# Layer 1 of a two-layer attention kernel: products, values and softmax sums in one TensorE tile mode

## The chip, the cores and the metric

The kernel runs on one core of a Trainium2 chip. The metric is the time of one execution in device microseconds (us). Before the change it is 3169.02 us, the median of three runs (3168.06 to 3169.51).

## The reference

The input x is one image of 256 x 256 tokens with 128 channels, fp32. Two layers are computed, each on a group-normalised copy of x and added to x. What the functions below leave out is the scaling of inputs and the reshapes between image and rows.

```python
# layer 0: rows of 256 tokens, 8 heads of 32, with a gate and a bias from pairs
bias = jnp.einsum('nijz,zh->nhij', pair_repr, bias_proj)[:, None]
gate = jax.nn.sigmoid(msa_repr @ gate_proj)
q, k, v = jnp.split(msa_repr @ qkv_proj, 3, axis=-1)
sim = jax.nn.softmax(jnp.einsum('nsqhc,nskhc->nshqk', q, k) * scale, axis=-1) + bias
out = (jnp.einsum('nshqk,nskhc->nsqhc', sim, v) * gate).reshape(bs, s, r, cm) @ out_proj

# layer 1: rows of 256 tokens, 4 heads of 64, each token sees 16 to either side
qkv = x2 @ w_in.T + b_in
q, k, v = (heads(t) for t in jnp.split(qkv, 3, axis=-1))
scores = jnp.einsum('bhid,bhjd->bhij', q, k) / jnp.sqrt(D)
scores = jnp.where(jnp.abs(i - j) <= band, scores, -jnp.inf)      # band = 16
out = jnp.einsum('bhij,bhjd->bhid', jax.nn.softmax(scores, axis=-1), v)
y = out.transpose(0, 2, 1, 3).reshape(B * T, F, C) @ w_out.T + b_out
```

In both layers a row has 256 tokens and 256 channels, and there are 128 rows (S = 128, R = C = 256). All arithmetic is in fp32.

## The kernel before

Layer 0 takes the first 2090 us of the span and is not touched by the change; a final check of the softmax sums follows layer 1. Names in the code: P is 128 (partitions), A is 4, B is 32, KB is 64 (keys of one block of the band), NB is 4 (such blocks in a row), and `strip(n)` is the partitions 32n to 32n + 31.

**Products of a row.** A 256 x 256 by 256 x 256 product is not done as eight quarter products but as seven, of sums and differences of quarters (`Seven`, and in layer 1 `Summed`). `Quarters` holds the weights' quarters and their sums. The sums of the inputs are made by GpSimd (`row_sums`: tile 1ts from 1xn for q and k, tile 1att from 1at for the output product o). Each of the seven products is one call of `nc.tensor.matmul` with a 128 x 128 stationary operand and 256 moving columns (L594). An fp32 matmul shows in the trace as two matmuls and two weight loads. `in_turn` takes the three streams q, k and o together: product n of q, of k, of o, each followed at once by its take (L655 to L685: a copy or an addition from PSUM, by ScalarE for q and k, by VectorE with the residual for o, by VectorE for the additions). That gives 21 products in a pass, named p1q, p1k and p1o.

**One pass of layer 1** works on two rows; the loop is `for i in range(last)` and runs 63 times. A pass counts here from its first p1q. In it TensorE does, in this order:

- the 21 products of `stretch`: q and k of the next pair of rows, o of an earlier pair;
- `values` (L1045): the values v of the next two rows, p1v, token by channel. Two column halves of the array, 128x64, take the keys of the two halves of a block of 64 tokens for half of the heads each, over four blocks and two input halves, with 128 moving columns;
- `scores` (L1066): 1sim, in 64x64 tiles with 96 moving columns, band blocks only. ScalarE then takes exponentials (L1074), GpSimd masks them (L1076, tile 1p) and adds those of even and odd blocks (L1083, tile 1zp);
- `attend` (L1107): 1av of the pair before, in 64x64 tiles, then 1zs (L1119): the sums of the softmax weights over keys, by a stationary operand `place` of zeros and ones. Each half of the partitions of 1zp is a half of the heads and goes to its own bank, in eight 64x32 tiles; `place` has ones in columns 0 to 15 for the lower half and 16 to 31 for the upper half, so that each bank holds the sums of one half of the heads and zeros for the other.

ScalarE copies the first bank of 1zs to 1z (L1130), and VectorE adds the second (L1131). VectorE takes reciprocals in three parts (L1144), the second and third between the takes of the next products. Then SyncE sends them to DRAM (L1152, rz_far) and back, spread over partitions (L1156, 1near), and loads a coming pair of rows (L741, yg). VectorE multiplies 1av with 1near (L1176, 1at), and 1av, of which there is one buffer, is free again. VectorE's transposes (L1219) and SyncE's stores (L1229) follow for finished rows.

**What sets the order.** In layer 1 the whole order on all engines is written out (`manual_schedule`): instructions run on each engine in the order of the program's text, and waits are placed where tiles demand them. PSUM banks for products and values come from a ring, here of four (`psum(lay, "1", 4, 0)`, L972); the other four banks are 1av's two and 1zs's two.

The last rows, after the loop, use `one_by_one` (L708, 1po) for their output product, with plain quarter products.

Of the kernel before, what the change touches and what calls it, by code (L numbers as in the profile page):

```python
# [9 lines left out]
F32 = mybir.dt.float32  # L10
# [29 lines left out]
def conv_preact_kernel(  # L40
# [525 lines left out]
    def row_sums(t, x, engine):  # L566
# [3 lines left out]
        engine.tensor_tensor(t[:, 2], x[:, 3], x[:, 2], ALU.subtract)  # L570
        engine.tensor_tensor(t[:, 3], x[:, 1], t[:, 1], ALU.subtract)

    class Seven:


        def __init__(self, pool, weights, x, t, name, tag, by_token=False):
            self.weights, self.x, self.t, self.by_token, self.name = weights, x, t, by_token, name
# [7 lines left out]
        def product(self, n, two=None, first=False):  # L585
            x, t = self.x, self.t
            moving = {1: x[:, 0], 2: x[:, 1], 3: x[:, 3], 4: t[:, 3], 5: t[:, 0], 6: t[:, 1], 7: t[:, 2]}[n]
            out = two if n == 2 else self.ps[:, 1 if n in (3, 5) else 0, :]

            first = first or n == 1  # L590
            flags = dict(stop=n in (2, 3, 4), skip_group_check=True)
            weights = self.weights.stationary(n)
            if not self.by_token:
                nc.tensor.matmul(out, lhsT=weights, rhs=moving, start=first, **flags)  # L594
                return
            for t2 in range(2):
                cols = slice(t2 * P, (t2 + 1) * P)
                nc.tensor.matmul(out[:, cols], lhsT=moving[:, cols], rhs=weights, start=first and t2 == 0, **flags)  # L598

        def take(self, what):  # L600
            if what == "15":
# [44 lines left out]
            p.add_mid()  # L646

    class Summed(Seven):

# [47 lines left out]
            if n in (1, 5):  # L699
                amid(n)  # L700

    def one_by_one(w, at, name, done):

        ps = proj_bank(name)
        done(ps)
        for m in range(2):
            for kt in range(2):
                nc.tensor.matmul(  # L708
                    ps[:, m, :], lhsT=w[:, kt, m * P : (m + 1) * P], rhs=at[:, kt, :],
                    start=(kt == 0), stop=(kt == 1),  # L710
                )
                yield
# [10 lines left out]
    with ExitStack() as both:  # L723
# [20 lines left out]
        with ExitStack() as lay0:  # L744
# [140 lines left out]
            def stretch(names, i, s, rest=lambda: None):  # L885

                po = iter(())
                if s >= 0:
                    po = one_by_one(out_sb, st[s]["at"], f"po{s}", lambda ps: st[s].update(po=ps))
                if 2 * i >= S:  # L890
                    rest()
                    for _ in po:
                        pass
                    return
                f, g = (
                    Seven(row, quarters[w], xns[i], tss[i], f"{w}{i}", w, by_token=(w == "v")) for w in names
                )
                for w, p in zip(names, (f, g)):
                    res[w, i] = p.to
                two_of_them(row, f, g, f"{names}{i}", po, rest)  # L900


            with tc.manual_schedule(engines={mybir.EngineType.PE, mybir.EngineType.Activation, mybir.EngineType.DVE}):
                for s in range(2):
                    normal(s)
                sum_rows(0)
                stretch("qk", 0, -1)
                for s in range(2, 4):
                    normal(s)
                stretch("vg", 0, -1)  # L910
                sum_rows(1)
                most1 = Most(st1, stats1, 3, 1)
                for s in range(S):
                    scores(s, 0)()
                    zs = sum_heads(s - 1)
                    join_tiles(s, 0, 0)
                    divide(s - 1, zs)
                    if s % 2 == 0:
                        e = res["g", s // 2]
                        nc.scalar.activation(e, e, AF.Exp, scale=-1.0)  # L920
                    z = hd[s - 1, "z"][0] if s > 0 else None
                    rest = ((0, 2), (1, 0), (1, 2))
                    if s < S - 1:
                        attend(s - 1)
                        last_exp = scores(s, 1)
                        if s == 4:
                            for weights in quarters1.values():
                                weights.sum()
                        stretch(("qk", "vg")[s % 2], s // 2 + 1, s - 1, last_exp)
                        for half, j in rest:  # L930
                            join_tiles(s, half, j)
                        least(s - 1, z)
                        if s >= S - 3:
                            most1.join(s - S + 3)
                        normal(s + 4)
                        if s % 2 == 1:
                            sum_rows((s + 3) // 2)
                        finish(s - 1)
                    else:

                        scores(s, 1)()
                        for half, j in rest:
                            join_tiles(s, half, j)
                        least(s - 1, z)
                        attend(s - 1)
                load1(0)
                load1(1)
                warm = proj_bank("warm")

                def keep_on(n):  # L950

                    for _ in range(n):
                        nc.tensor.matmul(warm[:, 0, :], lhsT=ident, rhs=out_sb[:, 0, :], start=True, stop=True)

                divide(S - 1, sum_heads(S - 1))
                last_z = hd[S - 1, "z"][0]
                attend(S - 1)
                for s in (S - 2, S - 1):
                    if s == S - 1:
                        keep_on(4)  # L960
                    for _ in one_by_one(out_sb, st[s]["at"], f"po{s}", lambda ps: st[s].update(po=ps)):
                        pass
                    finish(s)
                mean1, rstd1 = channel_columns(st1, most1, 1, keep_on)
                least(S - 1, last_z)
# [3 lines left out]


        with ExitStack() as lay:
            ps_av = psum(lay, "1", 4, 0)  # L972
            row = lay.enter_context(tc.tile_pool(name="row1", bufs=4))
            att = lay.enter_context(tc.tile_pool(name="att1", bufs=2))
            st, hd, outs = {s: {} for s in range(S)}, {}, {}
# [38 lines left out]
            def project(s):  # L1014

                if s < 0:
                    return iter(())
                return one_by_one(w_out_t, st[s]["at"], f"1po{s}", lambda ps: st[s].update(po=ps))

            ats, ats_t, outputs, last_ots = {}, {}, {}, {}  # L1020

# [15 lines left out]
            def values(s):  # L1037
                if s >= S:
                    return
                i, r = divmod(s, 2)  # L1040
                ps = proj_bank(f"p1v{s}").rearrange("p a (b c) -> p (a b) c", c=P)
                for b in range(NB):
                    for kt in range(2):
                        for half in range(2):
                            nc.tensor.matmul(  # L1045
                                ps[KB * half : KB * (half + 1), b, :],
                                lhsT=xns[i][:, 2 * r + kt, KB * b : KB * (b + 1)],
                                rhs=w_in_t[:, kt, 2 * C + P * half : 2 * C + P * (half + 1)],
                                start=(kt == 0), stop=(kt == 1),
                            )  # L1050
                v = row.tile([P, NB, P], F32, tag="v", name=f"1v{s}")
                nc.scalar.copy(v, ps)  # L1052
                st[s]["v"] = v
# [32 lines left out]
            def attend(i):  # L1086
# [6 lines left out]
                    av = [av[:, half] for half in range(2)]  # L1093
                else:
                    av = [proj_bank(f"1av{i}_{half}") for half in range(2)]
                zs = ps_av.tile([P, 2, 2, R], F32, tag="zs", name=f"1zs{i}", bufs=1)
                zps = []
                for r in range(2):
                    (p, zp), v = hd.pop(2 * i + r), st[2 * i + r]["v"]
# [13 lines left out]
                                )  # L1113

                for r in range(2):
                    for half in range(2):
                        for j in range(2):
                            keys = slice(KB * half, KB * (half + 1))
                            nc.tensor.matmul(  # L1119
                                zs[strip(2 * j + r), half, 0, :], lhsT=place[keys, :], rhs=zps[r][keys, j, :],  # L1120
                                start=True, stop=True,
                            )
                hd["av", i] = (av, zs)

            def sums(i):
                if i < 0:
                    return
                zs = hd["av", i][1]
                z = att.tile([P, R], F32, tag="z", name=f"1z{i}")
                nc.scalar.copy(z, zs[:, 0, 0, :])  # L1130
                nc.vector.tensor_tensor(z, zs[:, 1, 0, :], z, ALU.add)  # L1131
                rz = att.tile([P, R], F32, tag="rz", name=f"1rz{i}")
                near = att.tile([P, 2, 2, R], F32, tag="near", name=f"1near{i}", bufs=1)
                hd["z", i] = (z, rz, near)
# [388 lines left out]
```

## Time and profile before

| What | Value |
|---|---|
| Median of three runs | 3169.02 us |
| Span of the profiled execution, first to last instruction | 3173.6 us (4.6 us above the median; the profile gives no other time of that execution) |
| Layer 0 | 0 to about 2092 us |
| The 63 passes of layer 1 | 2092.7 to about 3122 us, 16.37 us each at the median |
| TensorE matmuls and weight loads | 36,859 each |
| TensorE, VectorE, ScalarE, GpSimd busy in 2092 to 3122 us | 1025, 661, 550 and 736 us of 1030 |
| 1near transfers | 124 of 256 KB |
| Granted TensorE clock | 0.991 |

A profile's line of a group gives line, engine, operation, the tile written and the tiles read, the tile mode (rows*columns), the shape of the operand and the count, then busy time and mean duration, then the idle time before it and what ended that. Starts are measured; ends of matmuls are modelled, so that the distance from start to start tells the cost of a matmul, and its duration doesn't. "issue" as a releaser means that the profile shows nothing that the engine waited for. In the list of DMA queues q8 and q14 carry instructions of the engines, and q1 data.

### The profile page before, as it was taken

How to read it: one execution, taken by the hardware profiler on the slowest of the kernel's cores; microseconds unless marked ns; L12 is line 12 of the kernel's file. 1: busy time of each engine (PE TensorE's matmuls, PEld its weight loads, DVE VectorE, ACT ScalarE, POOL GpSimd, SP SyncE). 2: the span in 40 equal slices, each digit the busy share in tenths (PEclk: the TensorE clock that was granted, in tenths of full speed). 3: DMA queues.
4: the chain of work that ended last, by engine and by line, in shares of the span. 5: the costliest groups of instructions: out<-in, count | busy, mean ns of one | idle time of the engine just before them, and what ended most of it. 6: DMA issues, size and time to landing. Idle time of an engine off the chain costs nothing.

```text
span 3173.6 us, 87645 instructions
## 1 busy us (share of the span) xinstructions
PE 3097.4 (98%) x36859; PEld 2384.0 (75%) x36859; DVE 2558.2 (81%) x4140; ACT 1870.3 (59%) x4064; POOL 1613.4 (51%) x1651
## 2 busy tenths in 40 slices
PE   7889999999999999999999999999999999999997
PEld 5567777777777777777777777768888888888886
DVE  4669999999999999999999999956666666666665
ACT  4656666666666666666666666645555555555553
POOL 3034444444444444444444444347777777777774
PEclk8989999999999999999999999999999999999999
DMA  9931111111111111111111111004444444444343
GB/s 379 424 109 42 41 41 34 41 35 39 37 35 41 35 39 37 38 38 35 41 34 37 39 37 39 28 28 102 96 101 101 93 99 102 100 97 101 91 100 69
DMA packets 357105, 242.44 MB, mean 76 GB/s; under 512 B 276072, under 2 KB 342112, under 8 KB 350560
## 3 DMA queue, kind: packets, MB, share of 16 engines
q1 hardware_dynamic: 355808, 234.39, 27.1%
q8 instruction: 292, 4.78, 0.6%
q0 software_dynamic: 752, 2.36, 0.2%
q14 instruction: 109, 0.89, 0.1%
q10 hardware_dynamic: 144, 0.00, 0.0%
HBM read 169.09 MB, written 67.62 MB: 75 GB/s over the span
## 4 chain that ended last, share of the span: by engine, by line
PE 91%; DMA 5%; DVE 2%; ACT 1%; issue 0%; POOL 0%; SPq 0%; DVEq 0%; POOLq 0%; ACTq 0%
PE sim L784 9%; PE p1v L1045 7%; PE po L708 7%; PE av L816 7%; PE bv L816 7%; PE p1q L594 6%; PE pv L598 6%; PE p1o L594 6%; PE pq L594 6%; PE p1k L594 6%; PE pk L594 5%; PE pg L594 5%; DMA pr<-in_L_conv_pair_repr_dram 4%; PE zs L830 4%; PE 1sim L1066 3%; PE 1av L1107 3%
## 5 line engine op out<-in xcount | busy, mean ns | idle before, releaser
L797 ACT ACTIVATE ex<-sim 128x512 f32<-128x512 f32 x1024 | 547.5, 605 | 429.9 <-PE sim L784 429.9
L806 DVE TENSOR_TENSOR both<-ex 128x512 f32<-128x512 f32 x512 | 483.9, 984 | 77.0 <-ACT ex L797 77.0
L846 DVE RECIPROCAL d<-d 128x512 f32<-128x512 f32 x128 | 429.2, 3353 | 4.4
L611 POOL TENSOR_TENSOR v<-v,twovg 128x256 f32<-128x256 f32 x64 | 75.4, 1179 | 548.0 <-ACT twovg L630 548.0
L784 PE MATMUL sim<-q,k 32*128 32x256 f32 x4096 | 295.7, 401 | 1.1 <-ACT ex L797 1.1
L708 PE MATMUL po<-at,out_sb 128*128 128x256 f32 x1024 | 285.0, 382 | 4.0 <-DVE at L864 4.0
L784 PEld LDWEIGHTS sim<-q,k 32*128 32x128 f32 x4096 | 186.7, 184 | 102.4 <-issue 95.0
L816 PE MATMUL bv<-bias_sb,v 128*32 128x256 f32 x4096 | 244.5, 379 | 0.7 <-DVE t L861 0.7
L816 PE MATMUL av<-ex,v 128*32 128x256 f32 x4096 | 244.5, 379 | 0.0
L1045 PEld LDWEIGHTS p1v<-w_in_t,1xn 128*64 128x64 f32 x4096 | 222.3, 137 | 21.5 <-PE p1k L594 20.2
L1045 PE MATMUL p1v<-w_in_t,1xn 128*64 128x128 f32 x4096 | 237.7, 274 | 0.3 <-POOL place L980 0.3
L1076 POOL TENSOR_TENSOR 1p<-1ex,seen 128x768 f32<-128x768 f32 x127 | 230.9, 1818 | 13.4 <-ACT 1ex L1074 13.4
L668 ACT ACTIVATE 1q<-p1q,bqk 128x256 f32<-128x256 f32 x192 | 91.1, 474 | 244.4 <-PE p1q L594 244.4
L708 PEld LDWEIGHTS po<-at,out_sb 128*128 128x128 f32 x1024 | 185.7, 191 | 25.4 <-issue 4.3
L1176 DVE TENSOR_TENSOR 1at<-1av,1near 128x512 f32<-128x512 f32 x128 | 82.6, 686 | 148.6 <-DMA 1near<-rz_far 116.7
L816 PEld LDWEIGHTS bv<-bias_sb,v 128*32 128x32 f32 x4096 | 133.2, 110 | 88.7 <-issue 1.1
L611 POOL TENSOR_TENSOR q<-q,twoqk 128x256 f32<-128x256 f32 x64 | 47.6, 744 | 298.5 <-ACT twoqk L630 298.5
L816 PEld LDWEIGHTS av<-ex,v 128*32 128x32 f32 x4096 | 133.2, 110 | 87.8 <-issue 0.3
L766 DVE TENSOR_SCALAR xn<-xt,mean,rstd 128x256 f32<-128x256 f32 x256 | 179.9, 742 | 0.0
L1083 POOL TENSOR_TENSOR 1zp<-1p 128x512 f32<-128x512 f32 x127 | 162.1, 1276 | 10.0
L568 POOL TENSOR_TENSOR 1ts<-1xn 128x256 f32<-128x256 f32 x64 | 47.0, 734 | 234.3 <-ACT 1xn L1006 234.3
L1052 ACT COPY 1v<-p1v 128x512 f32<-128x512 f32 x128 | 75.1, 587 | 135.1 <-PE p1v L1045 131.6
(300 smaller groups left out, 7872.4 us busy)
## 6 DMA issues: line engine op xcount, KB each, us to landing
pr<-in_L_conv_pair_repr_dram SPq DMA_DIRECT2D x32, 1024.0 KB
xs<-in_x_dram SPq DMA_DIRECT2D x16, 2048.0 KB
x<-o SPq DMA_DIRECT2D x64, 512.0 KB
yg<-x SPq DMA_DIRECT2D x64, 512.0 KB
out_dram<-1o SPq DMA_DIRECT2D x256, 128.0 KB
xg<-in_x_dram SPq DMA_DIRECT2D x252, 128.0 KB
1near<-rz_far SPq DMA_DIRECT2D x124, 256.0 KB
rz_far<-1rz SPq DMA_DIRECT2D x124, 4.0 KB
```

Of the source, the lines that this page charges most:

```text
L594: nc.tensor.matmul(out, lhsT=weights, rhs=moving, start=first, **flags)
L598: nc.tensor.matmul(out[:, cols], lhsT=moving[:, cols], rhs=weights, start=first and t2 == 0, **flags)
L708: nc.tensor.matmul(ps[:, m, :], lhsT=w[:, kt, m * P : (m + 1) * P], rhs=at[:, kt, :], start=(kt == 0), stop=(kt == 1),)
L766: nc.vector.tensor_scalar(xns[i][:, 2 * r + half, :], xt[:, half, :], mean0[:, half : half + 1], rstd0[:, half : half + 1], op0=ALU.subtra ...
L784: nc.tensor.matmul(sims[j][:, kt, :], lhsT=k[p0 : p0 + D0, 2 * r + half, kt * P : (kt + 1) * P], rhs=q[p0 : p0 + D0, 2 * r + half, :], sta ...
L797: nc.scalar.activation(ex[:, j], sims[j], AF.Exp, scale=1.0 / math.sqrt(D0))
L806: nc.vector.tensor_tensor(both[:, j : j + 2], ex[:, j : j + 2, 0, :], ex[:, j : j + 2, 1, :], ALU.add)
L816: nc.tensor.matmul(to[D0 * j : D0 * (j + 1), half, :], lhsT=v[:, 2 * r + half, c0 : c0 + D0], rhs=weights(4 * half + j, kt), start=(kt == ...
L846: nc.vector.reciprocal(d, d)
L1045: nc.tensor.matmul(ps[KB * half : KB * (half + 1), b, :], lhsT=xns[i][:, 2 * r + kt, KB * b : KB * (b + 1)], rhs=w_in_t[:, kt, 2 * C + P * ...
L1076: engine.tensor_tensor(p.rearrange("p j (r c) -> p (j r) c", c=WROW)[:, :, 0 : 2 * WSTEP] .rearrange("p r (t c) -> p r t c", c=WSTEP)[:, : ...
L1083: engine.tensor_tensor(zp, p[:, :, 0:R], p[:, :, R : 2 * R], ALU.add)
```

## The change

In layer 1 the products, the values and the sums of softmax weights all use the tile mode 128x32, four tiles beside each other, each with a stationary operand of 32 columns:

- a helper `in_columns` splits a matmul into four of 32 columns. `Summed` has WIDTH = 32, so that each of the 21 products is four matmuls; `Seven`, which layer 0 uses, keeps 128. `one_by_one` takes the width as an argument: 128 in layer 0, 32 in layer 1;
- `values` writes the four strips of the partitions with four tiles of 32 tokens instead of two of 64;
- 1zs takes all 128 partitions as the contraction, with four matmuls of 32 columns in place of eight. The columns of `place` keep the two halves of the heads apart, so that one bank holds the sums of both. The addition at L1131 goes, and ScalarE's copy alone fills 1z;
- the bank that 1zs gives up goes to the ring, five instead of four.

The order of the instructions stays as written. In layer 1 a wait that sat on one matmul now sits on the first of its four.

```diff
+    def in_columns(out, lhsT, rhs, width, **flags):
+
+        for c0 in range(0, P, width):
+            cols = slice(c0, c0 + width)
+            nc.tensor.matmul(out[cols], lhsT=lhsT[:, cols], rhs=rhs, **flags)
+
     class Seven:
 
+        WIDTH = P
...
             if not self.by_token:
-                nc.tensor.matmul(out, lhsT=weights, rhs=moving, start=first, **flags)
+                in_columns(out, weights, moving, self.WIDTH, start=first, **flags)
                 return
...
     class Summed(Seven):
 
+        WIDTH = B
...
-    def one_by_one(w, at, name, done):
+    def one_by_one(w, at, name, done, width):
...
-                nc.tensor.matmul(
-                    ps[:, m, :], lhsT=w[:, kt, m * P : (m + 1) * P], rhs=at[:, kt, :],
+                in_columns(
+                    ps[:, m, :], w[:, kt, m * P : (m + 1) * P], at[:, kt, :], width,
                     start=(kt == 0), stop=(kt == 1),
                 )
...
-            ps_av = psum(lay, "1", 4, 0)
+            ps_av = psum(lay, "1", 5, 0)
...
-                        for half in range(2):
+                        for n in range(A):
+                            half, keys = n // 2, KB * b + B * (n % 2)
                             nc.tensor.matmul(
-                                ps[KB * half : KB * (half + 1), b, :],
-                                lhsT=xns[i][:, 2 * r + kt, KB * b : KB * (b + 1)],
+                                ps[strip(n), b, :],
+                                lhsT=xns[i][:, 2 * r + kt, keys : keys + B],
                                 rhs=w_in_t[:, kt, 2 * C + P * half : 2 * C + P * (half + 1)],
...
-                zs = ps_av.tile([P, 2, 2, R], F32, tag="zs", name=f"1zs{i}", bufs=1)
+                zs = ps_av.tile([P, 2, R], F32, tag="zs", name=f"1zs{i}", bufs=1)
...
                 for r in range(2):
-                    for half in range(2):
-                        for j in range(2):
-                            keys = slice(KB * half, KB * (half + 1))
-                            nc.tensor.matmul(
-                                zs[strip(2 * j + r), half, 0, :], lhsT=place[keys, :], rhs=zps[r][keys, j, :],
-                                start=True, stop=True,
-                            )
+                    for j in range(2):
+                        nc.tensor.matmul(
+                            zs[strip(2 * j + r), 0, :], lhsT=place, rhs=zps[r][:, j, :], start=True, stop=True
+                        )
...
-                nc.scalar.copy(z, zs[:, 0, 0, :])
-                nc.vector.tensor_tensor(z, zs[:, 1, 0, :], z, ALU.add)
+                nc.scalar.copy(z, zs[:, 0, :])
```

## The prediction

> **What bounds the kernel now.** I read the page first, for the busy shares and the chain that ended last.
>
> ```profile
> span 3173.6 us, 87645 instructions
> PE 3097.4 (98%) x36859; PEld 2384.0 (75%) x36859; DVE 2558.2 (81%) x4140; ACT 1870.3 (59%) x4064; POOL 1613.4 (51%) x1651
> q8 instruction: 292, 4.78, 0.6%
> PE 91%; DMA 5%; DVE 2%; ACT 1%; issue 0%; POOL 0%; SPq 0%; DVEq 0%; POOLq 0%; ACTq 0%
> ```
>
> TensorE is busy 98% of the span and carries 91% of the chain; the 5% of DMA lies at the start. So what counts is TensorE's time in layer 1, of which 63 passes last 16.37 us each. Queue q8 I keep for later: 292 packets of 16 KB, and TensorE ran 2 x 36,859 matmuls and weight loads and about 670 semaphore instructions, 74,387 in all. 74,387 / 292 is 255, so one q8 packet is a block of 256 TensorE instructions. Next, TensorE's waits in the passes (engine, line, waited for: total, times, longest).
>
> ```profile
> PE 1av L1107 <- DVE 1at L1176: 0.7, 2, 0.4
> PE 1av L1107 <- issue: 0.2, 1, 0.2
> ```
>
> Less than 3 us of waits in 1000: no other engine's lateness bounds the passes. Then TensorE's timeline over one pass (start, duration, engine, line, tile, shape).
>
> ```profile
> 2501.01 0.59 PE L594 MATMUL p1k<-1ts,sums_1k 128*128 128x256 f32 x2
> 2501.44 0.64 PE L594 MATMUL p1o<-1att,sums_1o 128*128 128x256 f32 x2
> 2501.92 0.59 PE L594 MATMUL p1q<-1ts,sums_1q 128*128 128x256 f32 x2
> ...
> 2505.41 0.59 PE L594 MATMUL p1o<-1at,sums_1o 128*128 128x256 f32 x2
> 2505.94 3.71 PE L1045 MATMUL p1v<-w_in_t,1xn 128*64 128x128 f32 x64
> 2509.58 1.56 PE L1066 MATMUL 1sim<-1q,1k 64*64 64x96 f32 x61
> ...
> 2511.64 1.30 PE L1107 MATMUL 1av<-1p,1v 64*64 64x96 f32 x54 [0.22 <-issue]
> 2512.87 0.66 PE L1119 MATMUL 1zs<-1zp,place 64*32 64x256 f32 x16
> 2513.46 0.70 PE L594 MATMUL p1q<-1xn,w_in_t 128*128 128x256 f32 x2
> 2514.00 0.59 PE L594 MATMUL p1k<-1xn,w_in_t 128*128 128x256 f32 x2
> ```
>
> Starts count here, since ends are modelled. Every fp32 product is two passes through the array, 0.43 us together, and a loss shows as a longer step: 0.48 after the sixth and seventh p1o, 0.53 from p1o to p1v, 0.54 for the first p1q. And in this pass 1av stopped for 0.47 us (2511.17 to 2511.64) "<-issue", which is no semaphore.
>
> [...] each change costs 0.09 to 0.14 us more than a steady step. [...] the trace's loads last 190, 137 and 110 ns for 128, 64 and 32 columns, 0.84 ns a column, so an uncovered load costs about 104, 51 or 24 ns here. [...]
>
> **Part by part.** Each q, k and o product is 4 matmuls of 32 columns instead of one. Layer 0 has the price: bv in 128x32 with 256 columns,
>
> ```profile
> 1509.52 1.91 PE L816 MATMUL bv<-bias_sb,v 128*32 128x256 f32 x32
> 1511.24 1.91 PE L816 MATMUL av<-ex,v 128*32 128x256 f32 x32
> ```
>
> 32 matmuls in 1.72 us, 216 ns per four, which is exactly one 128x128 pass. So 21 products stay at 9.07 us, but become 336 instructions at 27 ns where they were 84 at 108. The values (p1v) go from 64 to 128 matmuls of 128 columns. No row has 128x32 at 128 columns; I take today's time, 3.50 us (109 ns for each two become 109 for each four, 13.7 ns an instruction). Below, nothing speaks for a gain, since the columns streamed are the same; above, [...] 0 to 0.51 us a pass, kept for the range. 1zs falls from 16 to 8 pairs in the same 0.43 us.
>
> What falls away is changes of mode, since q, k, o, values and sums are then one mode: first p1q 240 ns (136 on its start, 104 for the load before its second pass), p1o to p1v 144 (93 and 51), and two late 128-column loads in the p1o stream 86 (43 each; a 32-column load is 80 ns shorter). That is 470[...]: 0.455 us a pass. p1v to sims and 1av to 1zs stay. Over 62 intervals -28.2 us, and the first three stretches, without p1o to wait behind, give -1.5.
>
> The DVE addition at L1131 (425 ns) stays off the path: DVE waits 2.2 us before it and later for the transfer 1near, 116.7 us in 50 waits. It moves the first part of the reciprocal, but parts two and three follow takes of p1q, p1k and p1o, so rz_far, 1near and 1at hardly move. ACT's copy waits on the same 1zs. The fifth bank of the ring saves nothing where TensorE waits for nothing. No DMA is added or moved past another in its queue. With a pass shorter by 0.46, 1av begins at 14.04 us of the pass instead of 14.37, and 1at, which frees its bank, ends there at 12.7 to 14.85: about 6.5 us of waits in place of 3.3, +3.
>
> So far -27. Now the instructions. A pass had 506 TensorE instructions (250 pairs and 6 semaphores), two blocks; it gets 870, 3.4 blocks. The window with the stalled pass's packet, 2.5 us long, says
>
> ```profile
> DMA  8998989999988953533519000000000030000011
> q8 instruction: 1, 0.02, 2.6%
> ```
>
> one packet, 2.6% of 16 engines for 2.5 us, so 1.04 us, in the midst of 1near and yg, which fill the DMA engines to nine tenths. It ran from 2509.35 to 2510.40, and its first instruction started at 2511.64, 1.25 us after its end. In another pass, 2560 instructions on (ten blocks), 1.43 us after the end came a smaller stall; nowhere in the passes is the lag under 1.25. So a block is usable about 1.35 us after its packet. Supply, counted from the instruction 256 ahead of the block: the packet starts 1.5 us later (mean of 11 passes, 0.2 to 2.8) if that instruction lies in the first half of p1v, which meets 1near and yg, 0.4 in the second half; it takes 1.1; with 1.35, 3.9 and 2.9 us. [...] I charge 0.4: 4.3 and 3.3.
>
> Cover is the time that 256 instructions take: today at least 2.64 us (sims and 1av at 10.3 ns, with 0.3 of mode changes), but mostly over 4, as half a block is p1v at 27 ns. After, p1v, sims and 1av are 512 instructions in 6.4 us, and each pass has just one block begun in p1v: cover 3.3 on average in its first half, 3.0 in its second. Stall 1.0 in half the passes, 0.3 in the other half; and in 3 passes of 10 a block begun in the last 80 instructions of q, k, o misses by some 0.6. Together 0.5 + 0.15 + 0.2 = 0.85 us a pass, 53 us over 62.
>
> Sum: 3173.6 - 28.2 - 1.5 + 3 + 53 = 3199.9 on the profile's own execution; its span lies 4.6 above the median of the runs, so **3195 us**.
>
> **Rivals.** (1) Instruction fetch keeps up: [...] the sum without the 53 is 3169 - 27 = 3142. For it: over 74,000 instructions lost 0.6 us this way, and layer 0 takes its blocks at 27 ns without a stall. Against: nowhere today do 512 instructions follow at 10 to 14 ns. This is the other side; it decides where supply falls under the cover of 3.0 to 3.3 us, that is if the packet isn't held up by 1near. (2) Half the stall, 0.45 us a pass: 28 - 27, 3170, no change. (3) Starvation feeds on itself: both the block begun in p1v and the one before it late, by 1.5 to 2 us a pass, as delays of 2.8 occur already: 3169 - 27 + 93 to 124, 3235 to 3266. (4) Fetch harmless, but p1v at 125 ns for four: 3142 + 32 = 3174; this is TensorE's own issue as the bound.
>
> **Numbers.** Main case 0.48 (3178 to 3215 its own range); fetch harmless 0.22; half stall 0.08; heavy starvation 0.14; dearer p1v alone 0.08. 0.2%, about what a measurement of this kernel tells from no change, is 6.3 us. Faster is (1) and a little of (2): 0.24; same, most of (2) and part of (4): 0.08; slower, the rest, 0.68. Range 3141 to 3240: it takes in most of (1) and the near end of (3).
>
> **What would show it.** In the profile after: first p1q to p1k 0.43 instead of 0.54, p1o to p1v about 0.43 and p1o steps of 0.43 without 0.48 show the modes saved; p1v in 3.5 us shows its price; "issue" gaps inside p1v, sims or 1av, after q8 packets that start late under 1near, show the starvation, with q8 near 380 packets. I am wrong if those gaps are absent (then 3142), or if they are there and a pass still comes out under 16.3 us; and if 1av's waits on 1at reach some 0.5 us a pass, rather than 0.1, the bound has moved to the transfer.

## The result, and the profile after

The changed kernel takes 3220.02 us, the median of four runs (3219.54 to 3224.32), beside 3169.27 us for the kernel before: a ratio of 1.0159, 95% interval 1.0145 to 1.0174. It is slower by 51 us, where the forecast was 26.

The profiled execution has a span of 3218.4 us, 44.8 more than that of before (this profile lies 1.6 us under the median of its runs, that of before 4.6 above its own). From the page, in the order in which the lines of before were shown:

```profile
span 3218.4 us, 111797 instructions
PE 3093.7 (96%) x48525; PEld 2250.4 (70%) x48525; DVE 2533.0 (79%) x4076; ACT 1870.9 (58%) x4064; POOL 1616.3 (50%) x1651
q8 instruction: 383, 6.28, 0.8%
PE 90%; DMA 5%; issue 2%; DVE 2%; ACT 1%; POOL 0%; SPq 0%; DVEq 0%; POOLq 0%; ACTq 0%
```

TensorE has 11,666 more matmuls and as many more weight loads, and is busy 4 us less. Queue q8 has 91 packets more, 256 instructions each. "issue" on the chain has gone from 0 to 2%. TensorE's waits in layer 1 (engine, line, waited for: total us, times, longest; L1055 is the values, L1076 1sim, L1117 1av, L577 the helper with the products) name it:

```profile
PE 1sim L1076 <- issue: 19.4, 25, 1.5
PE 1av L1117 <- issue: 13.6, 27, 0.9
PE p1v L1055 <- issue: 7.3, 14, 0.9
PE p1q L577 <- issue: 2.7, 7, 0.5
PE 1sim L1076 <- ACT 1ex L1084: 1.2, 1, 1.2
```

Idle time is counted here from the modelled end of a matmul; from start to start a stop costs about 0.25 us more. The one wait of 1.2 us that is put down to ScalarE falls at the same kind of place as the stops below. The wait of 1av for 1at, which I had expected to double to 6.5 us, is not in this list of matmuls; at the weight loads it is there still, hardly changed (see the part on the prediction). TensorE's timeline shows two stops within a pass:

```profile
2505.16 0.64 PE L577 MATMUL p1k<-1xn,sums_1k 128*32 128x256 f32 x8
2505.59 0.64 PE L577 MATMUL p1o<-1at,sums_1o 128*32 128x256 f32 x8
2506.02 3.27 PE L1055 MATMUL p1v<-w_in_t,1xn 128*32 128x128 f32 x112
2510.23 0.64 PE L1055 MATMUL p1v<-w_in_t,1xn 128*32 128x128 f32 x16 [0.94 <-issue]
2510.80 1.55 PE L1076 MATMUL 1sim<-1q,1k 64*64 64x96 f32 x64
2512.17 1.08 PE L1117 MATMUL 1av<-1p,1v 64*64 64x80 f32 x47
2513.92 0.54 PE L1117 MATMUL 1av<-1p,1v 64*64 64x96 f32 x17 [0.67 <-issue]
2514.40 0.64 PE L1127 MATMUL 1zs<-1zp,place 128*32 128x256 f32 x8
2514.85 0.61 PE L577 MATMUL p1q<-1xn,w_in_t 128*32 128x256 f32 x8
2515.28 0.61 PE L577 MATMUL p1k<-1xn,w_in_t 128*32 128x256 f32 x8
```

The changes of mode are saved as forecast: first p1q to p1k is 0.43 us (0.54 before), p1o to p1v 0.43 (0.53). What is new are stops in the middle of p1v and of 1av, 256 instructions apart, where TensorE waits for no semaphore.

All such stops can be placed by the number of the instruction at which they fall, counting all of TensorE's recorded instructions (matmuls, weight loads and those that wait for semaphores) from the start of the program. Normal is here the third quartile of the steps between the same two kinds of instruction. In passes 4 to 63, 94 steps last over 0.2 us more than that:

```
instruction number modulo 256    stops    us
193                                94    70.2
any other                           0     0.0
from the end of the last q8 packet to the stopped instruction's start: median 1.40 us,
10th to 90th percentile 1.26 to 1.52
```

Every one stands at the boundary of a block of instructions (the count doesn't begin with the first of a block, so the boundary is at 193 and not at 0), and TensorE goes on 1.4 us after that block's packet has ended. This is the lag of 1.25 to 1.43 us from which the forecast started.

From pass to pass (all from the traces, from first p1q to first p1q, us; "without stops" adds up the medians of the parts, taken where no stop falls; the last column is the mean less that, so it holds short delays too):

| Kernel | without stops | mean, from the 4th pass | stops in a pass |
|---|---|---|---|
| before | 16.37 | 16.44 | 0.07 |
| changed | 15.94 (median of the run without 1near) | 17.32 | 1.38 |

0.43 us of saving and 1.31 us more in stops make +0.88 us, and over 60 passes +52.6; the first three passes add 0.8, and the two profiles differ by -3.8 in layer 0 and by -4.8 after the last pass begins. That sums to the 44.8.

### The profile page after: what moved, and what is told of

Read it like the earlier page. It is cut to its first block, busy times and chain, and to the rows that moved or that the text cites. A ratio compares the mean times of both kernels' runs of the same rounds, so it can differ in the third digit from the quotient of the medians.

```text
span 3218.4 us, 111797 instructions
## 1 busy us (share of the span) xinstructions
PE 3093.7 (96%) x48525; PEld 2250.4 (70%) x48525; DVE 2533.0 (79%) x4076; ACT 1870.9 (58%) x4064; POOL 1616.3 (50%) x1651
## 4 chain that ended last, share of the span: by engine, by line
PE 90%; DMA 5%; issue 2%; DVE 2%; ACT 1%; POOL 0%; SPq 0%; DVEq 0%; POOLq 0%; ACTq 0%
PE sim L793 9%; PE p1v L1055 7%; PE po L577 7%; PE av L825 7%; PE bv L825 7%; PE p1q L577 6%; PE p1o L577 6%; PE pv L577 6%; PE p1k L577 6%; PE pq L577 6%; PE pk L577 5%; PE pg L577 5%; PE zs L839 4%; PE 1sim L1076 3%; DMA pr<-in_L_conv_pair_repr_dram 3%; PE 1av L1117 3%
## 5 line engine op out<-in xcount | busy, mean ns | idle before, releaser
L577 PE MATMUL po<-at,out_sb 128*128 128x256 f32 x1024 | 285.1, 382 | 4.0 <-DVE at L873 4.0
L1150 DVE RECIPROCAL 1rz<-1z 128x64 f32<-128x64 f32 (+1 forms) x192 | 129.7, 678 | 183.3 <-ACT 1z L1137 183.3
L1055 PE MATMUL p1v<-w_in_t,1xn 128*32 128x128 f32 x8192 | 243.2, 273 | 7.9 <-issue 7.3
L1055 PEld LDWEIGHTS p1v<-w_in_t,1xn 128*32 128x32 f32 x8192 | 231.0, 110 | 20.5 <-issue 12.4
L577 PEld LDWEIGHTS po<-at,out_sb 128*128 128x128 f32 x1024 | 185.8, 192 | 25.3 <-issue 4.3
```

The lines of the kernel that those rows point to most:

```text
L577: nc.tensor.matmul(out[cols], lhsT=lhsT[:, cols], rhs=rhs, **flags)
L1055: nc.tensor.matmul(ps[strip(n), b, :], lhsT=xns[i][:, 2 * r + kt, keys : keys + B], rhs=w_in_t[:, kt, 2 * C + P * half : 2 * C + P * (half ...
L1150: nc.vector.reciprocal(rz[:, cols], z[:, cols])
```

## The experiments

Three questions: are the stops due to narrow tiles or to the density of instructions; what holds the blocks up; and what are the other parts worth? Each run's interval is that of its ratio to the kernel before, timed beside it (3170 to 3171 us).

**Values wide again**

```diff
-                        for n in range(A):
-                            half, keys = n // 2, KB * b + B * (n % 2)
+                        for half in range(2):
                             nc.tensor.matmul(
-                                ps[strip(n), b, :],
-                                lhsT=xns[i][:, 2 * r + kt, keys : keys + B],
+                                ps[KB * half : KB * (half + 1), b, :],
+                                lhsT=xns[i][:, 2 * r + kt, KB * b : KB * (b + 1)],
```

> The changed kernel with the values back in 128x64 tiles: 742 TensorE instructions a pass instead of 870, the values at 27 ns an instruction instead of 13.7. Theory (instruction blocks arrive late where 512 instructions follow within 6.4 us): the stalls of some 1.2 us a pass all but vanish, to under 0.2 us, as in the kernel before; the changes of mode around the values come back, 0.15 us a pass, so about 3155 to 3165 us, faster than before. Rival (narrow tiles for the products are what costs): most of the loss stays, 3200 us or more.

3151.85 us, ratio 0.9938 (0.9921 to 0.9954). TensorE's waits in the passes hold one stop over 0.5 us:

```profile
PE 1av L1116 <- issue: 1.0, 1, 1.0
PE p1q L577 <- DVE 1q L684: 0.3, 1, 0.3
```

With 742 instructions a pass, half as many again as before, the stops are back to 0.06 us a pass. It came out 3 us better than the range given. The narrow products, which bring 252 of the 364 added instructions, cost nothing.

**Values narrow alone**

```diff
 (the kernel before)
-                        for half in range(2):
+                        for n in range(A):
+                            half, keys = n // 2, KB * b + B * (n % 2)
                             nc.tensor.matmul(
-                                ps[KB * half : KB * (half + 1), b, :],
-                                lhsT=xns[i][:, 2 * r + kt, KB * b : KB * (b + 1)],
+                                ps[strip(n), b, :],
+                                lhsT=xns[i][:, 2 * r + kt, keys : keys + B],
```

> The kernel before with only the values in 128x32 tiles: 634 instructions a pass, of which 512 in the dense part. Theory: the stalls come with the values alone, 0.6 to 1.2 us a pass at block boundaries, 3205 to 3240 us. Rival (the total of instructions in a pass counts, 634 against 506): a quarter to a third of the stalls, 3180 to 3190 us.

3222.34 us, ratio 1.0154 (1.0137 to 1.0171). This one edit loses as much as the whole change. From its timeline:

```profile
2507.92 3.70 PE L1046 MATMUL p1v<-w_in_t,1xn 128*32 128x128 f32 x128
2511.55 0.40 PE L1067 MATMUL 1sim<-1q,1k 64*64 64x96 f32 x8
2513.49 1.39 PE L1067 MATMUL 1sim<-1q,1k 64*64 64x96 f32 x56 [1.54 <-issue]
```

The p1v itself takes 3.63 us where nothing stops it, as in 128x64 (3.64): four 32-column matmuls of 128 columns cost the 109 ns of two 64-column ones. So the tiles aren't slow; what follows them waits, 0.99 us a pass in the mean, and 73 of the 75 stops over 0.2 us stand at number 193 modulo 256, the other two just behind it. With 634 instructions a pass there are fewer blocks than with wide values (742) and some sixteen times the stops: here their number doesn't decide, their density does.

**No transfer of the reciprocals**

```diff
+            same_near = att.tile([P, 2, 2, R], F32, name="same_near", bufs=1)
+            nc.gpsimd.memset(same_near, 0.02)
...
-                near = att.tile([P, 2, 2, R], F32, tag="near", name=f"1near{i}", bufs=1)
+                near = same_near
+                if i >= last - 1:
+                    near = att.tile([P, 2, 2, R], F32, tag="near", name=f"1near{i}", bufs=1)
...
-                        if n == 5:
-                            by_transfer(i - 1)
```

> The changed kernel without the transfer of the reciprocals to DRAM and back in the passes: 1av is multiplied by a constant, so this part of the computation is left out. The loads yg and the stores stay. Theory that 1near holds the packets of instructions up by 1 to 2.5 us: stalls fall from 1.2 to 0.2 to 0.5 us a pass, 3155 to 3180 us. Rival (the fetch is too slow for the dense part even in idle DMA engines): stalls of 0.8 us or more stay, 3195 us or more.

3144.29 us, ratio 0.9914 (0.9898 to 0.9931), below the 3155 to 3180 given: the 3142 that the first rival had without stops, within 3 us, although TensorE has the same 870 instructions a pass in the same order. The stops fall from 1.38 to 0.14 us a pass, under the range given too. One thing more moved than I meant: yg, which stands behind 1near in SyncE's queue, is now issued some 9 us sooner, so this run takes both out of the values' way. Busy times by stretch for one pass each, the first half of p1v, its second half, and 1sim with 1av (the last three numbers of a line are granted clock, DMA share and GB/s); the changed kernel first, then this run:

```profile
2506.02:2507.90 1.88, 1.88 (x73) 1.88 (x69) 0.70 (x2) 1.29 (x4) 1.33 (x2) 1.00 0.99 221
2507.90:2510.80 2.90, 1.97 (x68) 1.50 (x60) 2.04 (x5) 0.59 (x1) 2.65 (x5) 1.00 0.43 134
2510.80:2514.40 3.60, 2.93 (x133) 2.65 (x129) 0.91 (x3) 2.22 (x5) 3.36 (x4) 1.00 0.45 78
```

```profile
2509.73:2511.50 1.77, 1.77 (x69) 1.76 (x65) 1.77 (x4) 1.29 (x4) 1.22 (x2) 1.00 0.03 9
2511.50:2513.37 1.87, 1.87 (x73) 1.67 (x64) 1.78 (x6) 0.59 (x1) 1.87 (x4) 1.00 0.00 0
2513.37:2516.10 2.73, 2.73 (x136) 2.64 (x134) 0.00 (x0) 2.23 (x5) 2.65 (x5) 1.00 0.58 100
```

In the changed kernel the DMA engines are 0.99 busy while the first half of the values runs; here 0.03. With the engines so idle, the same 512 dense instructions stop TensorE for 0.14 us a pass in place of 1.38. The packets themselves take 1.0 to 1.1 us in both kernels; what the data change is when they start.

**Early load of the coming rows**

```diff
+                    load1(i + 3)
                     stretch(i + 1, i - 2, amid)
```

> The changed kernel with the load of the coming rows (yg) issued at the start of the pass, ahead of the reciprocals' transfers in SyncE's queue, so that only 1near's 512 KB remain in the stretch in which the values begin. Theory (blocks are late behind data that the DMA engines move while the values run, whichever tile it is): the data end some 2 us earlier, blocks marked in the second half of the values and in 1sim come on time, stalls fall from 1.2 to 0.4 to 0.8 us a pass, 3170 to 3195 us. Rival (1near alone delays the blocks): no better than 3210 us. Rival (yg alone): about 3145 us.

3166.24 us, ratio 0.9984 (0.9976 to 0.9992), just below the range given; stops 0.52 us a pass. This separates the two transfers: 1near stays where it was and yg leaves. The same stretches:

```profile
2502.58:2504.40 1.82, 1.82 (x72) 1.81 (x68) 0.70 (x2) 1.29 (x4) 1.27 (x2) 1.00 0.47 108
2504.40:2506.22 1.82, 1.82 (x72) 1.62 (x61) 1.46 (x3) 0.59 (x1) 1.82 (x4) 1.00 0.03 9
2506.22:2508.91 2.69, 2.69 (x132) 2.60 (x128) 1.49 (x5) 2.23 (x5) 2.61 (x5) 1.00 0.11 22
```

0.47 of DMA in place of 0.99, and the packets of blocks marked (256 instructions ahead) in the first half of p1v start 0.56 us after the mark instead of 1.93; without both transfers 0.33. So both hold blocks up, and neither rival stands. Taking yg away gives 54 of the 76 us that both are worth; 1near taken away with yg left in place was not run, so the shares hold for this order alone. A large load moved by one line makes the changed kernel 54 us faster without touching TensorE's instructions.

Most of the stops that remain come behind another stop. In the second half of p1v the DMA engines are now all but idle (0.03), and still 19 of the 28 packets marked there start 1.18 us after the mark, and each of these blocks costs 0.70 us. These are the marks at which TensorE had itself just been stopped for a late block (they begin within 1.65 us of the end of their own packet). For the other 9 the packet starts after 0.38 us and the block costs 0.02. In the run without 1near, where none of these marks is late, it starts after 0.42 us in the mean. So here a block that comes late makes the next one late, in idle DMA engines too.

**One row's values ahead of the last three products**

```diff
-            if n in (1, 5):
+            if n in (1, 5, 4):
                 amid(n)
...
+                        if n == 4:
+                            values(s + 2)
+                            return
...
-                    values(s + 2)
                     values(s + 3)
```

> The changed kernel with the values of one of the two rows put ahead of the last three products, the others where they are: the same 870 instructions a pass, but the run at 14 ns or less shrinks from 512 to 384, and blocks marked in the values have products at 27 ns in their cover. Theory (cover decides): stalls fall from 1.2 to 0.3 to 0.7 us a pass, 3163 to 3190 us. Rival (the number of blocks in a pass decides, 3.4 as before): 3215 us or more.

3185.98 us, ratio 1.0046 (1.003 to 1.0063), as the theory had it: the same number of blocks and the same transfers, but a shorter dense run, and the stops fall to 0.74 us a pass, just above the 0.7 given.

**Both of these**

> The changed kernel with the values of one row put ahead of the last three products and yg issued at the start of the pass. Theory (stalls come where cover is short and data move): fewer stalls than with either edit alone, under 0.35 us a pass, 3143 to 3165 us. Rival (the two edits cure the same blocks): about 3166 us, as with the early load alone.

3158.51 us, ratio 0.9963 (0.9949 to 0.9977). Stops of 0.37 us a pass remain, against 0.52 and 0.74 with either edit: they add up in part, and the mean misses the 0.35 by a little. TensorE's waits:

```profile
PE 1av L1117 <- issue: 5.2, 12, 0.8
PE p1v L1055 <- issue: 1.5, 5, 0.5
PE 1zs L1127 <- issue: 1.4, 3, 0.5
```

Most of the rest sits in 1av, at the end of the dense run.

**Products and values in 64 columns**

```diff
     class Summed(Seven):
-        WIDTH = B
+        WIDTH = KB
 (and the values in 128x64 as above)
```

> Products and values in 128x64 tiles, 1zs in 128x32 as changed: 574 instructions a pass, the dense part 256 as before. Theory: stalls under 0.15 us a pass; the step from the products to the values saves 0.09 to 0.14 us a pass, the one from 1zs to the first product is smaller or equal to that of before: 3150 to 3168 us. Rival (narrow column tiles lose by themselves in the products): 3175 us or more without stalls at block boundaries.

3152.12 us, ratio 0.994 (0.9924 to 0.9957). The step from the products to the values is saved here without a dense run: products 9.19 us (9.35 before), and 574 instructions a pass, with 0.10 us of stops. From 1zs (128x32) to the first p1q takes 0.57 us, between the 0.59 of before and the 0.46 of one mode.

**The sums alone, with five banks and with four**

The kernel before with only the edits of `attend` and `sums`; the first has the ring of five, the second differs by one line.

```diff
-            ps_av = psum(lay, "1", 5, 0)
+            ps_av = psum(lay, "1", 4, 0)
```

> The kernel before with only 1zs in 128x32 tiles in one bank, without VectorE's addition and with five banks in the ring; products in 128x128, values in 128x64 as before. By the prediction these parts are worth nothing by themselves: 3166 to 3172 us. Rival (the wait before 1av and 1zs gets shorter without the addition, 0.09 us a pass as in the run with wide values): 3160 to 3166 us.

> The run with the sums alone, but with four banks in the ring as before (the bank that 1zs gives up stays unused). In that run a pass took 16.26 us at the median, 0.11 less than before, of which 0.09 between the first 1sim and the first 1zs. If the fifth bank saves the 0.09 (1sim of the second row no longer waits for a bank), it is back here: 16.34 us a pass and 3165 to 3169 us. If the narrow 1zs or the missing addition saves it: 16.26 us a pass and 3158 to 3163 us.

3160.33 us, ratio 0.9966 (0.9954 to 0.9979), with five banks; 3166.88 us, ratio 0.9989 (0.998 to 0.9998), with four. The first is faster than the prediction had these parts, the second within the range given for a saving by the fifth bank. A pass takes 16.26 and 16.35 us at the median. The two timelines differ in one place, first five banks, then four:

```profile
2500.00 3.71 PE L1054 MATMUL p1v<-w_in_t,1xn 128*64 128x128 f32 x64
2505.01 1.39 PE L1116 MATMUL 1av<-1p,1v 64*64 64x80 f32 x64
2506.34 0.64 PE L1126 MATMUL 1zs<-1zp,place 128*32 128x256 f32 x8
```

```profile
2506.74 0.23 PE L1116 MATMUL 1av<-1p,1v 64*64 64x80 f32 x1
2506.75 0.26 PE L1075 MATMUL 1sim<-1q,1k 64*64 64x96 f32 x3
2506.81 1.41 PE L1116 MATMUL 1av<-1p,1v 64*64 64x80 f32 x63
2508.15 0.64 PE L1126 MATMUL 1zs<-1zp,place 128*32 128x256 f32 x8
```

1av to 1zs is 1.33 us with five banks and 1.41 with four (from its first start), which is 0.09 us in nearly every pass. The difference begins at the first matmuls of the second row's 1sim: the kernel before and the run with four banks have three steps of 45, 24 and 83 ns where the run with five has 7, 63 and 7; 75 of the 89 ns are there. The fifth bank is worth 0.09 us a pass; the narrow 1zs and the missing addition the remaining 0.02, from 1zs to the first p1q.

**The early load elsewhere: on the kernel before, and with wide values**

> The kernel before with only yg issued at the start of the pass. Blocks of instructions cost it under 1 us and the wait of 1av for 1at 3 us, so both theories expect 3165 to 3170 us; a gain of more than 5 us would say that the gain of the run with wide values and an early yg comes from the load and not from the tiles.

> The changed kernel with the values in 128x64 tiles and yg issued at the start of the pass. The run with wide values alone had only 2 us of stalls left, so both theories expect little: 3145 to 3154 us.

3168.15 us, ratio 0.9989 (0.9982 to 0.9996), on the kernel before: its 0.07 us of stops and waits a pass are gone, and no more. With wide values 3146.41 us, ratio 0.9923 (0.9907 to 0.994), 24 us less than the kernel before and the best of the runs that do the whole computation. Not one step in its passes lasts over 0.12 us more than normal; a pass takes 16.09 us, median and mean. So its gain is that of the tiles, the sums and the fifth bank.

## Why the prediction was right, and where a term was off

**What bounds the kernel: right.** TensorE alone, before and after; each microsecond of stop is one of time.

**The saving in the modes: right in sum, 0.43 of 0.455 us a pass, by two errors that cancel.** First p1q and 1zs to p1q gave 241 ns (forecast 240), p1o to p1v 93 of 93, but the second part of that step only 10 of 51. The step on the p1o stream failed: the 86 ns of late loads were to vanish with loads 80 ns shorter. The trace has, for two steps of 475 ns before, three of 460, 468 and 468 after, two of them just ahead of p1o instead of behind it. A load shorter by 80 ns bought nothing, and what these steps wait for is not shown. The 15 ns between the forecast's 470 and 455 were an estimate of mine for the step to the sims and don't show: from the last p1v to the first 1sim it is 203 ns, 202 before (medians of 63 passes). Against that, the fifth bank was costed at nothing, "where TensorE waits for nothing", and is worth 89 ns. The list of waits doesn't show that wait: it is too short to leave TensorE idle by modelled ends, and is seen only from start to start.

**The values' price: right.** 109 ns for four (3.63 us a pass); the rival with 125 ns, an estimate of mine that no trace had shown, falls.

**1av's wait for 1at: wrong.** 3.3 us were to become 6.5. The trace shows this wait at the weight loads of 1sim that stand just ahead of 1av (who waited for 1at: total us, times), first the kernel before, then the changed one:

```profile
  PEld 1sim L1066: 3.1, 18
  PEld 1sim L1076: 3.4, 17
```

It didn't double, though in the changed kernel the stops give the other engines time. With wide values and hardly a stop it is 3.9 us in 23 waits. With wide values and the early load it does come to 6.3 us in 37 waits, yet a pass takes 16.09 us at the median with either number. These waits cost nothing that shows from start to start, so the 3 us were priced too high.

**Instruction blocks: 0.85 us a pass forecast and 1.38 measured, because one late block makes the next late.** The table goes by where the mark lies, that is the first instruction of the block ahead, 256 instructions before. A mark is late where TensorE had just been stopped at it. The unstopped cover is taken from the median pass of the run without 1near; supply is the delay of the packet after the mark, its own 1.1 us and the lag of 1.4.

| Mark in | mark | blocks in 60 passes | cover, unstopped | packet starts after | supply measured (forecast) | cost per block (forecast) | us in all |
|---|---|---|---|---|---|---|---|
| p1v, first half | on time | 32 | 3.46 | 1.98 | 4.44 (4.3) | 0.98 (1.0) | 31 |
| late in q, k, o | on time | 18 | 4.16 | 2.31 | 4.85 (not given) | 0.71 (0.6) | 13 |
| p1v, second half | on time | 9 | 3.14 | 1.48 | 3.95 (3.3) | 0.79 (0.3) | 7 |
| p1v, second half | late | 19 | 2.91 | 1.22 | 3.69 (3.3) | 0.76 (0.3) | 14 |
| 1sim | late | 31 | 3.61 | 1.41 | 3.93 (no stop) | 0.52 (0) | 16 |
| elsewhere | both | 95 | 6.1 | 1.6 | no stop | 0.01 | 1 |

Cost is the cover as it became, less the unstopped one; these sum to 82 us of the 83. The blocks with a mark on time cost 51 us, nearly the 53 forecast for all, and the first two rows are right one by one. The term that was mis-sized is the block that follows a late one: it was put at 0.3 us in the second half of p1v and at nothing in 1sim, and these two rows measure 30 us.

Data are a part of that: yg still fills 0.43 of the DMA engines in the second half of p1v of the pass shown, and the 9 marks on time there have 1.48 us, against 0.38 in the run with the early load. But of the late marks in 1sim and the second half of p1v, 29 have DMA engines under a tenth busy (from 0.5 us before the mark to the packet's start), and their packets still start 1.18 us after them. What holds them back is not shown. The 0.4 us that the forecast charged for a smaller head start in the dense stretch were an estimate of mine, and no trace shows that head start. What the run with the early load shows is a difference: after a late mark the packet starts 1.18 us on, after one on time 0.38, so 0.8 us later behind a stop, where I had charged 0.4. Late in q, k and o the cost was right.

**The rivals.** That blocks keep up was refuted for this kernel, and its number, 3142, was met when the transfers were gone (3144). Half the stops, 3170, was met by the early load (3166). The heavy case, in which a late block makes another late, had the mechanism that was seen; its 1.5 us a pass were nearly reached by the change itself, though the blocks that are late with it follow the one begun in p1v and don't precede it.

**Why the other side lost.** It was to win if supply fell under the cover of 3.0 to 3.3 us. In idle DMA engines it does, 2.8 us in both halves of p1v without 1near. With data in the way, or behind a block that was late itself, it doesn't.

## What to carry to other kernels

Before splitting matmuls into narrower tiles, count TensorE's instructions in the densest stretch and compare the time of 256 of them, the block seen here, with the time a block of instructions takes to come there, in the DMA traffic of that stretch: here 2.8 us in idle DMA engines and 3.9 to 4.9 behind data. The time of the matmuls themselves doesn't tell it: p1v took 3.63 us in narrow tiles and 3.64 in wide ones. Count a stop that does come more than once: here it took some 0.8 us from the next block. Where the changed kernel has 1.38 us of stops a pass (3220 us), widening one stretch left 0.06 (3152 us), and moving a bulk load out of it 0.52 (3166 us). Costs of less than a tenth of a microsecond in each pass, as the 89 ns of the fifth bank, are read from starts, not from the list of waits.

## What the runs showed of the hardware

TensorE stopped at 94 of the 204 block boundaries in passes 4 to 63, for 70 us, about 1.4 us after that one block's packet had ended. In none of the thirteen traces does a block's packet in these passes start more than about 0.7 us before TensorE begins the block ahead of it. Where 256 instructions lasted longer, 6.1 us in the last row of the table, a boundary cost 0.01 us; the supply measured was 2.8 us in idle DMA engines, 3.7 us in idle DMA engines after a block that was late itself, and 3.9 to 4.9 us behind data. I had expected loaded DMA engines to delay a packet of 16 KB; that moving one load of 512 KB per pass is worth 54 us, as much as the whole change cost, was more than I expected.
